# Layer 1's loop of a four-layer graph network: small results moved out of a shared PSUM bank, two sums moved to VectorE, and the steps of a turn put in another order

## The chip, the cores and the metric

The kernel is one program on one core of a Trainium2 chip. The core has five engines that run side by side, each through its own list of instructions in order: TensorE (PE, matmuls; its weight loads are listed as PEld), VectorE (DVE), ScalarE (ACT), GpSimd (POOL) and SyncE (SP, which here only starts DMA transfers). An engine waits on a semaphore until another has finished what it needs. Matmul results land in PSUM, everything else lives in SBUF. The metric is the device time of one execution in microseconds (us); before the change it was 1585.68 us, the median of three runs.

## The reference, cut to what matters

Eight batches of 2048 nodes with 64 features run through four graph layers, each closed by a residual sum and a layer norm. The change touches only layer 1:

```python
h = x @ W
# agg: for each of 64 hyperedges, a softmax-weighted sum of the h of its members
beta = sigmoid((h @ a_gn)[:, None, :] + (agg @ a_ge)[:, :, None])
all_he = elu(beta * h + (1 - beta) * agg)          # one row per (hyperedge, node) pair
industry = (adj / deg) @ (x @ W_ind)
coefs1 = softmax over a node's hyperedges of tanh(elu(agg) @ fcW + fcb) @ av
g = sum over hyperedges of coefs1 * all_he
pair = [industry, g]
coefs2 = softmax(tanh(pair @ fcW + fcb) @ av)       # two weights per node and batch
out = coefs2[0] * industry + coefs2[1] * g
x = layernorm(x + out)                               # over 64 features
```

A node belongs to few hyperedges. The kernel handles the first three memberships of each node as three "units", and further ones as a list of slots; unit 3 is such a slot, put back to its node by a matmul with a selection matrix `S`.

## The kernel before: the parts that the change touches

Layer 1's loop works on tiles of 128 nodes, 16 of them (`j` = 0 to 15); a tile is 128 partitions by 512 columns (8 batches of 64 features). Four generators describe the work on one tile: `units` (the gated hyperedge terms, result `g`), `industry` (the big product with the adjacency mask, 32 matmuls in 8 blocks of 4, each block one step `i`), and `mix_and_norm` (the two-way softmax and the layer norm). A string of steps says how one turn of the loop interleaves them; each engine then gets its instructions in exactly that order.

```python
bank = ps_s.tile([P, QW], F32, tag="bank", name="bank")        # ONE 128x512 PSUM tile for all small things
def units(j, dst):
    sm = bank[:, 208 * (j % 2):208 * (j % 2 + 1)]
    ...  # step sx: 3 small matmuls and a transpose of S[:, j] into sm
    nc.scalar.copy(ST, sm[:, 0:P])                             # step ST
    nc.scalar.copy(of_slot..., sm[:, P + 64:P + 80])
    ex = sm[:, P:P + 64]...                                    # step gates: 4 small VectorE ops read ex
    ...                                                        #   and write gate, coef (SBUF)
    tau = sm[:, 0:4 * B]...                                    # step tau: the gates' tanh goes BACK into the bank
    nc.scalar.activation(tau, gate, AF.Tanh, scale=0.5)
    for i in range(2):
        ...  # gp{i}: 4 matmuls into gp (2 banks, one buffer)
        # z{i}: three VectorE ops on 128x1024: d = h + 1 - gp ; d *= tau + 1 (reads the bank) ; d = d / 2 + gp
        # (for i = 1 the first two are on half, the other half comes from step t3: 8 ScalarE ops from dp)
        # exp{i}: ScalarE, gp <- exp(d - 1) ; e{i}: VectorE, ez <- max(min(gp, 1), d)
        # w{i}: GpSimd, ez *= coef (for i = 0 also g = ez[0] + ez[1])
    nc.gpsimd.tensor_tensor(g, g, w[1][:, 0], ALU.add)         # step g1
    nc.tensor.matmul(mv, ST, w[1][:, 1], ...)                  # step red
    nc.vector.tensor_tensor(g, g, mv, ALU.add)                 # step g
def mix_and_norm(j):
    nc.sync.dma_start(xr, kept[j])                             # step xg
    nc.gpsimd.tensor_tensor(r, g, xr, ALU.add)
    # for ind, then g: tr{i} 4 transposes, sT{i} ScalarE copy, fc{i} 2 matmuls (shown as 4), th{i} ScalarE tanh
    # sub: GpSimd, th[0] -= th[1]
    df, sw, s, rp = (bank[:, 416 + 48 * (j % 2) + k * B:][:, 0:B] for k in range(4))
    # df: 8 matmuls of one column into the bank ; sw: ScalarE tanh, bank to bank ; dlt: VectorE ind -= g
    # mix: VectorE: ind *= sw + 1 ; r += ind / 2 ; s = sum of r (into the bank) ; r -= s / 64 (reads the bank)
    # sq: ScalarE square ; var: VectorE sum ; rstd: GpSimd, 2 ops
    nc.scalar.copy(rp, rstd)                                   # step rp, into the bank
    nc.vector.tensor_tensor(x2[:, j, :], r, bcast(rp), ALU.mult)   # step x2
turns = (
    "u.gp0 u.z0 s.g1 s.red p.i o.df f.rstd m.xg s.g u.exp0 o.sw f.rp u.dp m.tr0 f.x2 "
    "u.e0 u.w0 o.dlt p.i u.gp1 u.t3 m.sT0 u.z1 p.i m.fc0 m.th0 u.exp1 o.mix v.sx v.ST "
    "o.sq m.tr1 m.sT1 p.i u.e1 u.w1 o.var v.gates v.tau p.i m.fc1 m.th1 m.sub p.i p.i p.i"
)
# in turn t:  p -> industry of t, u -> units of t+1, v -> units of t+2, s -> units of t,
#             m, o, f -> mix_and_norm of t-1, t-2, t-3
```

Of the kernel before, what the change touches and what calls it, by code (L numbers as in the profile page):

```python
# [18 lines left out]
P = 128  # L19
# [3 lines left out]
BC = B * C  # L23
# [26 lines left out]
def kernel(  # L50
# [53 lines left out]
    def b_view(t2):  # L104
        return t2.rearrange("p (b c) -> p b c", b=B)
# [299 lines left out]
    def layer1(  # L405
# [28 lines left out]
        with tc.tile_pool(name="fa", bufs=2) as fa, tc.tile_pool(  # L434
# [201 lines left out]
            for j in range(NT):  # L636
# [6 lines left out]
        fw = stack.enter_context(tc.tile_pool(name="fw", bufs=2))  # L643
        mjp = stack.enter_context(tc.tile_pool(name="mj1", bufs=2))
        turn = {}
        homes = {"g": (0, 1, 2, 3), "ind": (4, 5, 14), "sT": (6, 7), "r": (8, 9, 10),
                 "xr": (12,), "sq": (13,)}

        def row(tag, name):
            turn[tag] = turn.get(tag, -1) + 1  # L650
            home = homes[tag][turn[tag] % len(homes[tag])]
            return own.tile([P, BC], F32, tag=f"b1_{home}", name=name)

        def small(tag, name, shape=(P, B), bufs=2):
            return fw.tile(list(shape), F32, tag=tag, name=name, bufs=bufs)
# [4 lines left out]
        ps_g = stack.enter_context(tc.tile_pool(name="fg", bufs=1, space=PSUM))  # L660
        ps_m = stack.enter_context(tc.tile_pool(name="fm", bufs=2, space=PSUM))
        ps_s = stack.enter_context(tc.tile_pool(name="fs", bufs=1, space=PSUM))

        bank = ps_s.tile([P, QW], F32, tag="bank", name="bank")
        ps_acc = stack.enter_context(tc.tile_pool(name="fi", bufs=1, space=PSUM))
        ps_fc = stack.enter_context(tc.tile_pool(name="ff", bufs=1, space=PSUM))
        extv = ext.rearrange("p u k b -> p (u k b)")


        def units(j, dst):  # L670

            cols = slice(j * P, (j + 1) * P)
            sm = bank[:, 208 * (j % 2):208 * (j % 2 + 1)]

            for i in range(2):
                nc.tensor.matmul(
                    sm[:, P + 32 * i:P + 32 * i + 32], (oh01, oh23)[i][:, cols], extv,
                    start=True, stop=True,
                )
            nc.tensor.matmul(  # L680
                sm[:, P + 64:P + 80], S[:, j, :], hgr[:, j].rearrange("p k b -> p (k b)"),
                start=True, stop=True,
            )
            transpose(sm[:, 0:P], S[:, j, :])
            yield "sx"
            ST = small("ST", f"ST_{j}", (P, P), 3)
            nc.scalar.copy(ST, sm[:, 0:P])
            of_slot = small("of_slot", f"of_slot_{j}", (P, 2, B))
            nc.scalar.copy(of_slot.rearrange("p k b -> p (k b)"), sm[:, P + 64:P + 80])
            yield "ST"  # L690
            ex = sm[:, P:P + 64].rearrange("p (u k b) -> p u k b", u=4, k=2)
            gate = small("gate", f"gate_{j}", (P, 4, B))
            coef = small("coef", f"coef_{j}", (P, 4, B), 3)
            for t, k, op in ((gate, 0, ALU.add), (coef, 1, ALU.mult)):
                nc.vector.tensor_tensor(
                    t[:, 0:3, :], ex[:, 0:3, k, :],
                    hgr[:, j, k, :].unsqueeze(1).to_broadcast([P, 3, B]), op,
                )
                nc.vector.tensor_tensor(t[:, 3, :], ex[:, 3, k, :], of_slot[:, k, :], op)
            yield "gates"  # L700

            tau = sm[:, 0:4 * B].rearrange("p (u b) -> p u b", u=4)
            nc.scalar.activation(tau, gate, AF.Tanh, scale=0.5)
            tau3 = small("tau3", f"tau3_{j}")
            nc.scalar.activation(tau3, tau[:, 3, :], AF.Copy, bias=1.0)
            yield "tau"


            def per_b(t, u, n):
                return (  # L710
                    t[:, u:u + n, :].rearrange("p u b -> p (u b)").unsqueeze(2)
                    .to_broadcast([P, n * B, C])
                )

            def by_b(t):
                return t.rearrange("p u (b c) -> p (u b) c", b=B)

            w = []
            for i in range(2):
                gp = ps_g.tile([P, 2, BC], F32, tag="g", name=f"gp_{j}_{i}")  # L720
                for u in range(2):
                    rs = slice(u * 64, (u + 1) * 64)
                    for part in (agg_hi, agg_lo):
                        nc.tensor.matmul(  # L724
                            gp[:, u, :], r_((oh01, oh23)[i][rs, cols]), r_(part[rs]),
                            start=part is agg_hi, stop=part is agg_lo,
                        )
                yield f"gp{i}"
                d = small("d", f"d_{j}_{i}", (P, 2, BC))
                n = 2 - i  # L730
                if i == 1:
                    for b in range(B):
                        bc = slice(b * C, (b + 1) * C)
                        nc.scalar.activation(
                            d[:, 1, bc], dp[:, bc], AF.Copy, scale=tau3[:, b:b + 1]
                        )
                    yield "t3"
# [4 lines left out]
                nc.vector.scalar_tensor_tensor(  # L742
                    by_b(d[:, 0:n]), per_b(tau, 2 * i, n), 1.0, by_b(d[:, 0:n]),
                    op0=ALU.add, op1=ALU.mult,
                )
                nc.vector.scalar_tensor_tensor(d, d, 0.5, gp, op0=ALU.mult, op1=ALU.add)  # L746
                yield f"z{i}"
                nc.scalar.activation(gp, d, AF.Exp, bias=minus1)
                yield f"exp{i}"
                if i == 0:  # L750

                    dp = ps_m.tile([P, BC], F32, tag="m", name=f"dp_{j}")
                    nc.tensor.matmul(dp, S[:, j, :], h_sb[:, j, :], start=True, stop=False)  # L753
# [5 lines left out]
                    yield "dp"  # L759
                ez = small("ez", f"ez_{j}_{i}", (P, 2, BC))  # L760
# [30 lines left out]
        def mix_and_norm(j):  # L791
# [31 lines left out]
            df, sw, s, rp = (  # L823
                bank[:, 416 + 48 * (j % 2) + k * B:][:, 0:B] for k in range(4)
            )
            for b in range(B):
                nc.tensor.matmul(  # L827
                    df[:, b:b + 1], th[0][:, b % 2, (b // 2) * P:(b // 2 + 1) * P], av_sb,
                    start=True, stop=True,
                )  # L830
# [10 lines left out]
            nc.vector.scalar_tensor_tensor(  # L841
                b_view(r), bcast(s), -1.0 / C, b_view(r), op0=ALU.mult, op1=ALU.add
            )
# [25 lines left out]
        second = "gp0 z0 exp0 dp e0 w0 gp1 t3 z1 exp1 e1 w1"  # L869
# [826 lines left out]
```

## Time and profile before

| what | value |
|---|---|
| time, median of 3 runs | 1585.68 us (1582.55 to 1592.32) |
| span of the profiled execution | 1586.5 us |
| PE busy, share of the span | 1396.5 us, 88% |
| DVE busy | 897.3 us, 57% |
| ACT busy | 296.4 us, 19% |
| POOL busy | 347.6 us, 22% |
| granted TensorE clock, whole span | 0.905 |
| layer 1's loop, from the first block of the mask product to layer 2 | about 869 to 1280 us |

How to read it. Busy time is an average over stages that have different limits, so it says little about one stage. A busy PE is not a PE at full speed, as its clock is granted in two levels and the same matmul takes longer at the lower one. A group line names the kernel's line, the engine, the operation and the tiles (out<-in). "Idle before" is the time in which that engine stood still just before the instruction, and "<-" names whose end let it go on. A line of the stage table gives the stage, its length, the busy time of each engine in it (with the number of instructions in brackets), the granted clock, and the DMA's share and rate.

### The profile page before, as it was taken

Reading aid. Unit: us, or ns where it says so; the run is one execution under the profiler, and the core shown is the slowest. Engines: PE = TensorE matmul, PEld = TensorE weight load, DVE = VectorE, ACT = ScalarE, POOL = GpSimd, SP = SyncE. Lnnn points to the kernel's source line nnn. Section 1 sums busy time; section 2 is a strip of 40 time slices with the busy share of each in tenths; the row PEclk is TensorE's granted clock in tenths of the full one; section 3 lists DMA queues with packets and bytes.
Section 4 is the critical chain, followed back from the end, with each engine's and each line's share of the span. In section 5 each row is a group of like instructions: output and inputs, shape, how many; then the busy total and the mean of one; then the engine's idle time right before and its main releaser. Section 6 shows DMA issues by size and latency. Waiting matters only on the chain.

```text
span 1586.5 us, 19276 instructions
## 1 busy us (share of the span) xinstructions
PE 1396.5 (88%) x7552; PEld 1074.8 (68%) x7552; DVE 897.3 (57%) x1627; ACT 296.4 (19%) x700; POOL 347.6 (22%) x245
## 2 busy tenths in 40 slices
PE   6877959999999999994877988888888879999997
PEld 4666748888888888882654555555555568888886
DVE  6655405665665666575764555555555466565554
ACT  2100100001001000001331433333333322111111
POOL 3344411011000100000001535353545432000000
PEclk9989979999999999995995977788787889999999
DMA  7555191112212211002001212121212032343562
GB/s 266 225 212 212 53 207 55 48 55 74 60 52 64 74 48 33 22 8 51 1 7 54 67 33 67 34 67 33 67 34 67 7 80 81 109 130 107 173 185 95
DMA packets 166707, 131.51 MB, mean 83 GB/s; under 512 B 12208, under 2 KB 151888, under 8 KB 162256
## 3 DMA queue, kind: packets, MB, share of 16 engines
q1 hardware_dynamic: 146496, 100.68, 21.4%
q10 hardware_dynamic: 19872, 28.94, 5.3%
q8 instruction: 62, 1.02, 0.3%
q0 software_dynamic: 240, 0.56, 0.1%
q14 instruction: 37, 0.30, 0.1%
HBM read 104.99 MB, written 25.17 MB: 82 GB/s over the span
## 4 chain that ended last, share of the span: by engine, by line
PE 68%; DVE 11%; issue 3%; DMA 2%; ACT 2%; POOL 1%; ACTq 1%; SPq 0%; DVEq 0%; POOLq 0%
PE pp L175 20%; PE a L927 15%; PE ind L927 7%; PE y2p L927 7%; PE hp L556 2%; PE bank L827 2%; PE u L1031 2%; DVE d L742 2%; DVE d L738 2%; PE gp L724 2%; PE trm L149 1%; PE fc L815 1%; PE try L149 1%; DVE d L746 1%; PE dp L753 1%
## 5 line engine op out<-in xcount | busy, mean ns | idle before, releaser
L186 DVE SCALAR_TENSOR_TENSOR r<-pp,emb_sb,r 128x256 f32<-128x256 f32 x512 | 247.7, 484 | 107.9 <-PE pp L175 94.1
L175 PE MATMUL pp<-w_sb,xT 64*128 64x256 f32 x1024 | 157.6, 382 | 16.6 <-DMA xT<-in_xt 14.2
L175 PE MATMUL pp<-w_sb,y1T 64*128 64x256 f32 x1024 | 157.4, 381 | 0.0
L175 PE MATMUL pp<-w_sb,y2T 64*128 64x256 f32 x1024 | 155.7, 378 | 0.0
L927 PE MATMUL ind<-y_hi,mj_l 128*128 128x512 f32 x256 | 133.0, 520 | 0.0
L175 PEld LDWEIGHTS pp<-w_sb,xT 64*128 64x128 f32 x1024 | 100.0, 188 | 32.5 <-DMA xT<-in_xt 14.6
L351 PE MATMUL y1p<-x_hi,m 128*128 128x512 f32 x256 | 107.7, 421 | 10.9 <-DVE m L318 10.9
L927 PE MATMUL ind<-y_lo,mj_l 128*128 128x512 f32 x256 | 116.9, 457 | 0.0
L351 PE MATMUL y1p<-x_lo,m 128*128 128x512 f32 x256 | 107.0, 418 | 4.1 <-DVE x_lo L301 4.1
L175 PEld LDWEIGHTS pp<-w_sb,y2T 64*128 64x128 f32 x1024 | 101.7, 188 | 9.6
L175 PEld LDWEIGHTS pp<-w_sb,y1T 64*128 64x128 f32 x1024 | 100.5, 188 | 10.5 <-issue 0.5
L763 POOL TENSOR_TENSOR ez<-ez,coef 128x1024 f32<-128x1024 f32 x32 | 65.8, 2056 | 184.8 <-DVE ez L761 125.7
L738 DVE SCALAR_TENSOR_TENSOR d<-h,gp 128x1024 f32<-128x1024 f32 (+1 forms) x32 | 30.6, 955 | 132.5 <-PE gp L724 132.5
L927 PE MATMUL y2p<-y_hi,mj_y 128*128 128x512 f32 x256 | 103.4, 404 | 0.4 <-DMA mj_y<-mask 0.4
L927 PE MATMUL a<-y_lo,mj_l 128*128 128x512 f32 x256 | 103.5, 405 | 0.0
L927 PE MATMUL a<-y_hi,mj_l 128*128 128x512 f32 x256 | 102.8, 402 | 0.0
L927 PE MATMUL y2p<-y_lo,mj_y 128*128 128x512 f32 x256 | 102.5, 400 | 0.0
L341 POOL TENSOR_TENSOR ms<-m,sb 128x2048 f32<-128x2048 f32 x16 | 78.6, 4912 | 106.7 <-ACT sb L331 68.9
L927 PE MATMUL a<-v_hi,mj_l 128*128 128x512 f32 x256 | 99.9, 391 | 0.0
L927 PE MATMUL a<-v_lo,mj_l 128*128 128x512 f32 x256 | 99.7, 390 | 0.0
L927 PEld LDWEIGHTS ind<-y_hi,mj_l 128*128 128x128 f32 x256 | 59.6, 233 | 35.1 <-issue 23.9
L953 POOL TENSOR_TENSOR y<-y_hi,y_lo 128x512 f32<-128x512 f32 x16 | 20.5, 1284 | 265.2 <-PE try L149 265.0
(246 smaller groups left out, 2354.1 us busy)
## 6 DMA issues: line engine op xcount, KB each, us to landing
mj_l<-mask SPq DMA_DIRECT2D x192, 256.0 KB, 3.9
raw<-in_at SPq DMA_DIRECT2D x16, 1024.0 KB, 5.9
mask<-m ACTq DMA_DIRECT2D x16, 1024.0 KB, 5.9
mj_y<-mask SPq DMA_DIRECT2D x64, 256.0 KB, 3.9
xraw<-in_xn SPq DMA_DIRECT2D x4, 1024.0 KB, 6.3
xs<-in_xn SPq DMA_DIRECT2D x16, 256.0 KB, 2.9
xT<-in_xt ACTq DMA_DIRECT2D x16, 256.0 KB, 2.9
kept<-x SPq DMA_DIRECT2D x16, 256.0 KB, 2.0
```

The costliest lines, as they stand in the source:

```text
L149: nc.tensor.matmul(dst, src, ident, start=True, stop=True, is_transpose=True)
L175: nc.tensor.matmul(pp[:, h, pl, :], src[rs, 2 * bq + pl, ncols], w_sb[rs, k, dq * 4 * C:(dq + 1) * 4 * C], start=k == 0, stop=k == K - 1,)
L186: nc.vector.scalar_tensor_tensor(rb, ppv[:, :, dd, :], emb_sb[:, j, d:d + 1], rb, op0=ALU.mult, op1=ALU.add,)
L341: nc.gpsimd.tensor_tensor(ms, m, sb[:, qc].unsqueeze(1).to_broadcast([P, 4, QW]), ALU.mult)
L351: nc.tensor.matmul(accs[jj], r_(m[:, mm, jj * P:(jj + 1) * P]), r_(part[:, 4 * kk + mm, :]), start=i == 0 and mm == 0 and part is x_hi, st ...
L556: nc.tensor.matmul(mm[:, i, 0:2 * P + 4], xT[:, 2 * p2 + i, :], wb, start=True, stop=True)
L724: nc.tensor.matmul(gp[:, u, :], r_((oh01, oh23)[i][rs, cols]), r_(part[rs]), start=part is agg_hi, stop=part is agg_lo,)
L738: nc.vector.scalar_tensor_tensor(d[:, 0:n], h_sb[:, j, :].unsqueeze(1).to_broadcast([P, n, BC]), 1.0, gp[:, 0:n], op0=ALU.add, op1=ALU.sub ...
L742: nc.vector.scalar_tensor_tensor(by_b(d[:, 0:n]), per_b(tau, 2 * i, n), 1.0, by_b(d[:, 0:n]), op0=ALU.add, op1=ALU.mult,)
L763: nc.gpsimd.tensor_tensor(by_b(ez), by_b(ez), per_b(coef, 2 * i, 2), ALU.mult)
L827: nc.tensor.matmul(df[:, b:b + 1], th[0][:, b % 2, (b // 2) * P:(b // 2 + 1) * P], av_sb, start=True, stop=True,)
L927: nc.tensor.matmul(acc, r_(a[:, mt, :]), r_(part[:, mt, :]), start=mt == 0 and part is hi, stop=mt == NT - 1 and part is lo,)
```

## The change

It keeps the arithmetic's result and alters where small things lie, which engine does some of them, and the order of a turn:

- The shared bank is gone. The small matmuls of `sx` and of `df` each get a PSUM tile of their own time (one buffer for both in turn). ScalarE copies all 80 small columns to SBUF at once (`ex`); the gates, their tanh (`tau`, now in place over `gate`), `sw`, the norm's sum `s` and `rstd` stay in SBUF.
- Two GpSimd sums go to VectorE: the last sum of `g` and the residual's sum with `xr`.
- The last product of the norm (`x2`) goes from one VectorE op to eight ScalarE ops (one per batch, with `rstd` as the scale), and the copy `rp` goes.
- `t3` comes before `e0`, `mix` is cut into `mult`, `r` and `centre`, one block of the mask product stands between `fc0` and `sx`, and the row `xr` is loaded a turn earlier into one of two buffers.

```diff
-        homes = {"g": (0, 1, 2, 3), "ind": (4, 5, 14), "sT": (6, 7), "r": (8, 9, 10),
-                 "xr": (12,), "sq": (13,)}
+        homes = {"g": (0, 1, 2, 3), "ind": (5, 14), "sT": (7, 4), "r": (8, 9, 10),
+                 "xr": (6, 12), "sq": (13,)}
-        bank = ps_s.tile([P, QW], F32, tag="bank", name="bank")
-            sm = bank[:, 208 * (j % 2):208 * (j % 2 + 1)]
+            sm = ps_s.tile([P, QW], F32, tag="sm", name=f"sx_{j}")
-            of_slot = small("of_slot", f"of_slot_{j}", (P, 2, B))
-            nc.scalar.copy(of_slot.rearrange("p k b -> p (k b)"), sm[:, P + 64:P + 80])
+            ex = small("ex", f"ex_{j}", (P, 5, 2, B))
+            nc.scalar.copy(ex.rearrange("p u k b -> p (u k b)"), sm[:, P:P + 80])
-            ex = sm[:, P:P + 64].rearrange("p (u k b) -> p u k b", u=4, k=2)
-            tau = sm[:, 0:4 * B].rearrange("p (u b) -> p u b", u=4)
+            tau = gate
 ... (d2 for i = 1 is taken early, so that step t3 can run after dp and before e0)
-            nc.gpsimd.tensor_tensor(g, g, w[1][:, 0], ALU.add)
-            yield "g1"
-            nc.vector.tensor_tensor(g, g, mv, ALU.add)
+            nc.vector.tensor_tensor(w[1][:, 0], w[1][:, 0], mv, ALU.add)
+            nc.vector.tensor_tensor(g, g, w[1][:, 0], ALU.add)
-            r = row("r", f"r1_{j}")
-            nc.gpsimd.tensor_tensor(r, g, xr, ALU.add)
-            yield "xg"
+            yield "xr"
-            df, sw, s, rp = (
-                bank[:, 416 + 48 * (j % 2) + k * B:][:, 0:B] for k in range(4)
-            )
+            df = ps_s.tile([P, QW], F32, tag="sm", name=f"df_{j}")[:, 0:B]
+            sw = small("sw", f"sw_{j}")
-            nc.vector.scalar_tensor_tensor(r, ind, 0.5, r, op0=ALU.mult, op1=ALU.add)
+            yield "mult"
+            r = row("r", f"r1_{j}")
+            nc.vector.scalar_tensor_tensor(r, ind, 0.5, g, op0=ALU.mult, op1=ALU.add)
+            nc.vector.tensor_tensor(r, r, xr, ALU.add)
+            yield "r"
+            s = small("s", f"s_{j}")
-            yield "mix"
+            yield "centre"
-            nc.scalar.copy(rp, rstd)
-            yield "rp"
-            nc.vector.tensor_tensor(b_view(x2[:, j, :]), b_view(r), bcast(rp), ALU.mult)
+            for b in range(B):
+                bc = slice(b * C, (b + 1) * C)
+                nc.scalar.activation(x2[:, j, bc], r[:, bc], AF.Copy, scale=rstd[:, b:b + 1])
-            "u.gp0 u.z0 s.g1 s.red p.i o.df f.rstd m.xg s.g u.exp0 o.sw f.rp u.dp m.tr0 f.x2 "
-            "u.e0 u.w0 o.dlt p.i u.gp1 u.t3 m.sT0 u.z1 p.i m.fc0 m.th0 u.exp1 o.mix v.sx v.ST "
-            "o.sq m.tr1 m.sT1 p.i u.e1 u.w1 o.var v.gates v.tau p.i m.fc1 m.th1 m.sub "
-            "p.i p.i p.i"
+            "m.xr u.gp0 s.red u.z0 f.rstd s.g p.i u.exp0 o.df o.sw u.dp m.tr0 u.t3 m.sT0 p.i u.e0 "
+            "u.w0 o.dlt o.mult u.gp1 f.x2 u.z1 p.i m.fc0 m.th0 u.exp1 o.r p.i v.sx v.ST m.tr1 "
+            "m.sT1 u.e1 u.w1 o.centre o.sq v.gates v.tau p.i m.fc1 p.i m.th1 m.sub p.i o.var p.i"
```

More of the change, by code (lines that the diff above doesn't have):

```diff
@@ L698, in units @@
                 )
-                nc.vector.tensor_tensor(t[:, 3, :], ex[:, 3, k, :], of_slot[:, k, :], op)
+                nc.vector.tensor_tensor(t[:, 3, :], ex[:, 3, k, :], ex[:, 4, k, :], op)
             yield "gates"
-            tau = sm[:, 0:4 * B].rearrange("p (u b) -> p u b", u=4)
+            tau = gate
             nc.scalar.activation(tau, gate, AF.Tanh, scale=0.5)
@@ L728, in units @@
                 yield f"gp{i}"
-                d = small("d", f"d_{j}_{i}", (P, 2, BC))
+                if i == 0:
+                    d, d2 = (small("d", f"d_{j}_{k}", (P, 2, BC)) for k in range(2))
+                else:
+                    d = d2
                 n = 2 - i
[L731 to L735, printed above, removed]
-                        )
-                    yield "t3"
                 nc.vector.scalar_tensor_tensor(
@@ L759, in units @@
                     yield "dp"
+                    for b in range(B):
+                        bc = slice(b * C, (b + 1) * C)
+                        nc.scalar.activation(
+                            d2[:, 1, bc], dp[:, bc], AF.Copy, scale=tau3[:, b:b + 1]
+                        )
+                    yield "t3"
                 ez = small("ez", f"ez_{j}_{i}", (P, 2, BC))
@@ L822, in mix_and_norm @@
             yield "sub"
-            df, sw, s, rp = (
-                bank[:, 416 + 48 * (j % 2) + k * B:][:, 0:B] for k in range(4)
-            )
+            df = ps_s.tile([P, QW], F32, tag="sm", name=f"df_{j}")[:, 0:B]
             for b in range(B):
@@ L854, in mix_and_norm @@
             yield "rstd"
-            nc.scalar.copy(rp, rstd)
-            yield "rp"
-            nc.vector.tensor_tensor(b_view(x2[:, j, :]), b_view(r), bcast(rp), ALU.mult)
+            for b in range(B):
+                bc = slice(b * C, (b + 1) * C)
+                nc.scalar.activation(x2[:, j, bc], r[:, bc], AF.Copy, scale=rstd[:, b:b + 1])
             yield "x2"
@@ L868, in layer1 @@
         first = "sx ST gates tau"
-        second = "gp0 z0 exp0 dp e0 w0 gp1 t3 z1 exp1 e1 w1"
+        second = "gp0 z0 exp0 dp t3 e0 w0 gp1 z1 exp1 e1 w1"
         turns = (
-            "u.gp0 u.z0 s.g1 s.red p.i o.df f.rstd m.xg s.g u.exp0 o.sw f.rp u.dp m.tr0 f.x2 "
-            "u.e0 u.w0 o.dlt p.i u.gp1 u.t3 m.sT0 u.z1 p.i m.fc0 m.th0 u.exp1 o.mix v.sx v.ST "
-            "o.sq m.tr1 m.sT1 p.i u.e1 u.w1 o.var v.gates v.tau p.i m.fc1 m.th1 m.sub "
-            "p.i p.i p.i"
+            "m.xr u.gp0 s.red u.z0 f.rstd s.g p.i u.exp0 o.df o.sw u.dp m.tr0 u.t3 m.sT0 p.i u.e0 "
+            "u.w0 o.dlt o.mult u.gp1 f.x2 u.z1 p.i m.fc0 m.th0 u.exp1 o.r p.i v.sx v.ST m.tr1 "
+            "m.sT1 u.e1 u.w1 o.centre o.sq v.gates v.tau p.i m.fc1 p.i m.th1 m.sub p.i o.var p.i"
         )
```

## The prediction

> **What bounds the kernel now.** I read first the stages, with one turn of layer 1's loop per stage. A turn starts where the first block of `gp` matmuls starts. Each row gives the stage and its length, then PE, PEld, DVE, ACT and POOL busy, the granted clock and the DMA.
>
> ```profile
> 881.73:899.03 17.30, 15.89 (x70) 9.47 (x69) 9.64 (x13) 8.31 (x19) 9.50 (x7) 1.00 0.27 77
> ...
> 1059.76:1086.21 26.45, 22.46 (x87) 13.53 (x86) 14.11 (x20) 9.22 (x22) 12.28 (x9) 0.81 0.18 50
> 1086.21:1111.41 25.20, 20.98 (x87) 13.39 (x86) 14.11 (x20) 9.31 (x22) 12.22 (x9) 0.86 0.18 53
> ...
> 1216.33:1238.56 22.23, 19.98 (x80) 12.32 (x80) 13.69 (x16) 8.61 (x18) 12.12 (x9) 0.85 0.21 60
> ```
>
> No other engine is busy for more than 14.11 of some 26 us, so PE's list sets the turn. Turns 2 to 13 run from 899.03 to 1216.33: 317.3 us, 26.44 each. Turn 1 (first row), which has no `df` and nothing of the residual and norm yet, takes 17.30 us at full clock. What fills the other 9? I asked what PE waited for in those twelve turns (total, times, longest):
>
> ```profile
> PE bank L676 <- DVE r L841: 38.2, 12, 3.5
> PE bank L827 <- DVE d L742: 9.3, 12, 0.8
> ```
>
> The first line is `sx` (it writes `bank`) waiting for the norm's centring, a VectorE op that reads its own eight columns of the same bank. The second is `df` waiting for the second op of `z0`, which reads `tau` in the bank. Neither is a dependence of data. That is 38.2/12 = 3.18 and 9.3/12 = 0.78, together 3.96 us a turn. The rest shows in PE's instructions of turn 8 (start, length, engine, what; the wait in brackets):
>
> ```profile
> 1062.08 0.39 PE L927 MATMUL ind<-y_lo,mj_l 128*128 128x512 f32 x1
> 1063.27 1.92 PE L827 MATMUL bank<-av,th 128*128 128x1 f32 x16 [0.80 <-DVE d L742]
> 1065.05 1.69 PE L753 MATMUL dp<-h,S 128*128 128x512 f32 x2
> ...
> 1070.01 0.63 PE L927 MATMUL ind<-y_lo,mj_l 128*128 128x512 f32 x1
> ...
> 1072.54 0.40 PE L927 MATMUL ind<-y_hi,mj_l 128*128 128x512 f32 x1
> 1073.10 1.13 PE L815 MATMUL fc<-sT,fcw_sb 64*128 64x512 f32 x4
> 1077.42 0.63 PE L676 MATMUL bank<-ext,oh 128*128 128x32 f32 x4 [3.19 <-DVE r L841]
> ...
> 1080.91 0.63 PE L927 MATMUL ind<-y_hi,mj_l 128*128 128x512 f32 x1
> 1081.33 0.63 PE L927 MATMUL ind<-y_lo,mj_l 128*128 128x512 f32 x1
> ```
>
> After each wait the same 128x512 matmul goes from 0.40 to 0.63 us (starts 0.43 apart, not 0.23). So a wait is paid twice: as idle time and as a slow clock after it.
>
> **What the Trainium skill says.** "PSUM — Partial Sum Buffer", section "PSUM bank collisions raise a hardware error": accesses of different engines have to be kept apart by bank, not by address. The trace agrees: `sx` at columns 0 to 415 waits 3.2 us for an op on columns above 416. "TensorE: Matmul & The Clock Gate", Part 1: the clock falls to half after a window of about 3.4 us without enough activity and rises after one busy window. The trace agrees: slow stretches follow the 3.2 us wait and the stretch of `df` with its wait, spacing 0.43 against 0.23. "ScalarE: Activation LUTs", section "What ACT_TABLE_LOAD costs": 186 ns, plus 93 for a pointer operand, plus 0.833 per element, less 93 of overlap back to back; for 64 columns I estimate 239 ns an op from it. The trace's eight alike ops (`d<-dp`) take 1.74 us, 218 each; I use that. "GPSIMD Engine Reference", section 3.1: a two-input elementwise op is about twice as slow there as on VectorE. Here 1278 ns against 681 for 128x512.
>
> **The change, part by part.**
>
> *The floor of a PE turn.* Turn 1 holds two waits, 1.04 us (`g`) and 0.37 (`e0`): 17.30 - 1.41 = 15.9. Add `df`: without a wait, in turn 15, it runs from 1240.53 to 1242.23, so 1.7. The block moved between `fc0` and `sx` makes one more change between the two kinds of matmul, each about 0.35 us of PEld "issue". Floor: 15.9 + 1.7 + 0.35 = 18.0 us. So the old average of 26.44 is 17.6 + 3.96 of waits + 0.2 more in `df` + some 4.7 of slow clock.
>
> *Removed.* With `tau`, `s`, `sw` and `rstd` in SBUF and `ex` copied by ScalarE, the tile of `sx` and `df` has readers on ScalarE alone: `sw` (done some 7 us before `sx`) and the two copies. Both waits go, 3.96 us a turn.
>
> *Moved between engines.* VectorE gains two sums of 0.69 and loses `x2` (0.69): 14.1 to 14.8 us. GpSimd loses 1.28 + 1.27: 12.2 to 9.7. ScalarE loses `rp` (0.17) and gains eight ops (1.74): 9.3 to 10.9. None reaches 18, so what counts is whether a chain through them is late.
>
> *The chains, laid out by hand at 18 us, from the start of `gp0`.* VectorE: `z0` 0.8 to 4.6 (three of 1.22, as now), the two sums of `g` to 5.9, under ScalarE's `exp0` (4.7 to 5.8), `e0` to 7.2. PE reaches `gp1` at about 7.5, so this just fits. ScalarE: `t3` from 6.1 to 7.9, `sT0` to 8.5 (`fc0` comes at 9.3), `x2` to 10.3, `th0` 10.5 to 11.6, `exp1` to 12.7 (`z1` ends at 11.35), the copies of `sx` and `sT1` to 13.75, `fc1` at 13.85: tight. VectorE: `r` to 12.75, `e1` 12.8 to 14.0, `centre` to 15.4, `gates` to 15.9. ScalarE: `sq`, `tau` to 16.4, `th1` to 17.55. GpSimd: `sub` (2.4) to 20.0; the next turn's `df` comes at 18.0 + 2.55 = 20.5. Nothing stands in PE's way for long, though four places have under 0.6 us to spare. I allow 0.4 us a turn.
>
> *Clock.* The slow stretch after `sx` has lost its cause. That after `df` may stay, as 16 one-column matmuls do little. In turn 14, with the wait, it came; in turn 15, where `df` followed without a wait, the matmuls after it still took 0.39. I expect it in about a third of the turns, 2.7 us each: 0.9.
>
> *Sum.* 18.0 + 0.4 + 0.9 = 19.3 us a turn, 7.1 less, over 12 turns 85 us. Turn 14 loses a wait of 0.78 and part of a slow stretch: -2. Turns 0 and 1 gain a change of matmul kind: +0.7. At the end of the loop layer 2's first copy on VectorE no longer stands behind the wait for the last `rstd` (2.09 us), but one VectorE sum was added: -1. Together -87: 1585.7 - 87 = 1499; I say 1500.
>
> **The rivals.**
>
> 1. *The slow clock stays.* If `df` alone sets it off in each turn, 2.7 us instead of 0.9: 18.0 + 0.4 + 2.7 = 21.1, 64 us saved, about 1520. For it: turn 14 had no wait at `sx`, and yet a clock of 0.85. Against: turn 15.
> 2. *A wait takes the place of the old one.* `gp1` on `e0`, `fc1` on `sT1` or `df` on `sub` could each be late by 0.5 to 1 us, most likely `fc1`: in turn 14 it waited 1.47 us for `sT1`. There `sq` stood ahead of `sT1`; in the new order it stands behind. If two are late by a microsecond, with half the slow stretches left: 18.0 + 2 + 1.5 = 21.5, 1525.
> 3. *The mask's load becomes late.* The load of `xr` stands ahead of the next mask in SyncE's list. Its buffer is free after `r` (12.75) only, where the mask's four loads now start at a turn's begin. Started at 13 and landing 3.9 us later, the first quarter is there at 17.5 to 18; it is needed at 19.2. So hidden, but with less to spare; if not, a wait of 1 to 2 us, 1525.
> 4. *VectorE becomes the bound.* At 14.8 of 18 us it is not, unless chains line up badly; that is rival 2.
>
> **Range and chances.** With no slow clock and no leftover wait the turn is 18.0: 12 x 8.4 + 2 = 103 saved, 1483. With rivals 1 and 2 together (22 us a turn) it is 1532. So 1482 to 1532. Staying within 2% (above 1554) needs a turn of over 23.8, which would keep two thirds of the loss: unlikely. Slower needs a new stall of over 10 us a turn, and nothing points at one. Faster by over 2%: 0.95; within: 0.04; slower: 0.01.
>
> **What the profile after will show.** Right: no PE wait for the centring or for `z0` at `sx` and `df`; turns 2 to 13 of 18 to 21 us; a clock of the loop above 0.90; VectorE near 14.8 us a turn; unchanged stages before 869 us. Wrong: turns above 22 us, PE waiting for `sT`, `sub` or the mask's load, or a clock still at 0.81 although the waits are gone.

## The result and the profile after

After the change the kernel takes **1522.08 us** (median of 4, 1519.46 to 1524.41); the kernel before took 1586.11 us in the same series (median of 4). The ratio is **0.9592**, 95% interval 0.9557 to 0.9627: 4.1% faster, some 64 us. The profiled execution spans 1522.7 us at a clock of 0.925 (before: 1586.5 us at 0.905).

The stages of the kernel after, one turn each, in the columns used before (stage and length, then PE, PEld, DVE, ACT and POOL busy, clock, DMA):

```profile
946.49:966.68 20.19, 17.96 (x86) 11.06 (x86) 18.85 (x22) 10.80 (x30) 11.05 (x6) 1.00 0.24 66
966.68:986.99 20.31, 18.07 (x87) 11.08 (x86) 19.07 (x22) 11.02 (x31) 11.05 (x6) 1.00 0.22 66
1007.27:1029.12 21.85, 21.18 (x86) 12.88 (x86) 18.95 (x22) 10.90 (x31) 11.04 (x6) 0.84 0.21 61
...
1049.31:1069.62 20.31, 19.62 (x87) 12.13 (x86) 19.08 (x22) 11.02 (x31) 11.05 (x6) 0.92 0.23 66
```

Turns 2 to 13 run from 905.63 to 1151.52: 245.9 us, 20.49 each, where they were 26.44. Compare the second row with the last: at a clock of 1.00 PE is busy for 18.07 us, at 0.92 for 19.62, and both turns take 20.31. PE has slack in the first and so no longer sets the turn. VectorE is busy for 19.1 us in both, not 14.8, though it does only what it was meant to do: 252 instructions in the twelve turns, 21 in each, where it was 20 (one that straddles the end of a turn is counted in both rows). Its own waits from 905 to 1130 us, eleven turns, (total, times, longest) leave it idle for some 1.5 us a turn:

```profile
DVE d L730 <- PE gp L720: 12.5, 13, 4.2
DVE var L848 <- ACT sq L845: 3.6, 10, 0.4
```

So **VectorE's list now bounds most turns**, though not by itself: the chain of the turn at 966.68 runs through VectorE's ops from 967.46 to 980.94, then through `exp1` and `sT1` on ScalarE to `fc1` (982.93) and 3 us of mask product on PE, back to the next `gp0`. PE's waits, from 840 to 1230 us, show both old bank waits gone and two for late results in their place:

```profile
PE df L820 <- POOL th L816: 10.6, 14, 1.7
PE fc L810 <- ACT sT L805: 9.9, 8, 1.9
```

Why does VectorE take longer? Here are lines from the turn at 966.68 of the kernel after (start, length, engine, what). Each VectorE op shown stands beside a GpSimd op:

```profile
967.79 2.38 POOL L816 TENSOR_TENSOR th<-th,th 128x1024 f32<-128x1024 f32 x1 [2.65 <-ACT th L813]
968.79 2.46 DVE L734 SCALAR_TENSOR_TENSOR d<-gate,d 128x1024 f32<-128x1024 f32 x1
970.12 1.22 POOL L850 TENSOR_SCALAR var<-var 128x8 f32<-128x8 f32 x1
970.22 1.95 PE L820 MATMUL df<-av,th 128*128 128x1 f32 x16 [0.68 <-POOL th L816]
975.05 2.28 POOL L761 TENSOR_TENSOR ez<-ez,coef 128x1024 f32<-128x1024 f32 x1 [1.96 <-DVE ez L759]
975.67 2.21 DVE L830 SCALAR_TENSOR_TENSOR ind<-sw,ind 128x512 f32<-128x512 f32 x1
982.93 1.13 PE L810 MATMUL fc<-sT,fcw_sb 64*128 64x512 f32 x4 [1.57 <-ACT sT L805]
983.53 1.90 POOL L761 TENSOR_TENSOR ez<-ez,coef 128x1024 f32<-128x1024 f32 x1 [4.48 <-DVE ez L759]
984.02 1.97 DVE L840 SCALAR_TENSOR_TENSOR r<-s,r 128x512 f32<-128x512 f32 x1
986.02 0.63 ACT L845 ACTIVATE sq<-r 128x512 f32<-128x512 f32 x1 [3.14 <-DVE r L840]
```

In the kernel before, the same four ops (`mult`, the centring and the second ops of `z0` and `z1`) took this long in turns 2 to 13 (count, then busy us, mean ns):

```profile
L742 DVE SCALAR_TENSOR_TENSOR d<-bank,d 128x1024 f32<-128x1024 f32 x12 | 14.7, 1225 | 1.2
L742 DVE SCALAR_TENSOR_TENSOR d<-bank,d 128x512 f32<-128x512 f32 x12 | 8.3, 691 | 0.5
L841 DVE SCALAR_TENSOR_TENSOR r<-bank,r 128x512 f32<-128x512 f32 x12 | 8.3, 691 | 0.4
L836 DVE SCALAR_TENSOR_TENSOR ind<-bank,ind 128x512 f32<-128x512 f32 x12 | 8.2, 685 | 0.0
```

The second op of `z0` (L734) starts at 968.79, inside GpSimd's `sub` (967.79 to 970.17), and ends at 971.25: 1.1 us after `sub`, as if it had begun only then. It took 1.22 before. The `mult` (L830) ends 0.55 us after `w0` and takes 2.21 instead of 0.69. The centring (L840) ends 0.56 us after `w1` and takes 1.97 instead of 0.69. With 1.01 instead of 0.69 for the half op of `z1` (mean of its group) that is 1.24 + 1.52 + 1.28 + 0.32 = **4.4 us in such a turn** (4.1 in the mean of the twelve, as `z0` is not always hit in full), which the profile counts as busy time. It goes the other way too: GpSimd's small addition to `var` (L850), issued while L734 runs, takes 1.22 us; alone it takes 0.24.

These four ops have one thing in common: their small operand (`tau`, `sw`, `s`) lay in PSUM before and lies in SBUF now. The Trainium skill, "SBUF — State Buffer", section "Who interferes with whom", says what that may do: a VectorE instruction with two inputs in SBUF contends with a GpSimd instruction that reads SBUF, not with one that only writes there, and whichever was issued first holds the shared port until it is done. One more hint is L836 (`r` + `xr`), which also reads two tiles in SBUF: at 981.57 GpSimd is idle, and it takes 0.69.

From there to PE's waits the way is short. A late centring makes `sq`, `th1` and `sub` late, so `sub` meets `z0` and `df` waits 0.68. A late `mult` pushes `z1` back, then `exp1` (ScalarE, 980.96), then `sT1` behind it, and `fc1` waits 1.57.

**Theory "ports".** The separation of banks took the old waits away; putting `tau`, `sw` and `s` into SBUF, of all places outside the bank, made VectorE share its way to SBUF with GpSimd, which stretches the chain through its list to 20.3 us, 2.3 above PE's floor. **Rivals:** the two sums that VectorE took over make its list too long; or the new order puts `sT1` and `sub` too late by itself; or `df` keeps the clock slow whatever is done.

### The profile page after: what moved, and what is told of

It is laid out like the page before. It is cut to its first block, busy times and chain, and to the rows that moved or that the text cites. A ratio compares the mean times of both kernels' runs of the same rounds, so it can differ in the third digit from the quotient of the medians.

```text
span 1522.7 us, 19336 instructions
## 1 busy us (share of the span) xinstructions
PE 1364.3 (90%) x7552; PEld 1051.2 (69%) x7552; DVE 965.9 (63%) x1643; ACT 323.3 (21%) x812; POOL 325.3 (21%) x213
## 4 chain that ended last, share of the span: by engine, by line
PE 63%; DVE 11%; ACT 4%; issue 3%; DMA 2%; POOL 2%; ACTq 1%; SPq 0%; DVEq 0%; POOLq 0%
PE pp L175 21%; PE a L925 15%; PE y2p L925 7%; PE ind L925 4%; PE hp L556 2%; PE u L1029 2%; DVE d L734 2%; PE fc L810 1%; PE try L149 1%; PE df L820 1%; POOL th L816 1%; DVE ind L830 1%; DVE d L738 1%; DVE d L730 1%; PE yp L1055 1%
## 5 line engine op out<-in xcount | busy, mean ns | idle before, releaser
L175 PE MATMUL pp<-w_sb,xT 64*128 64x256 f32 x1024 | 158.3, 383 | 18.5 <-DMA xT<-in_xt 16.1
L925 PE MATMUL ind<-y_hi,mj_l 128*128 128x512 f32 x256 | 118.5, 463 | 0.7 <-ACT ind L783 0.7
L351 PE MATMUL y1p<-x_hi,m 128*128 128x512 f32 x256 | 107.5, 420 | 10.7 <-DVE m L318 10.7
L925 PE MATMUL ind<-y_lo,mj_l 128*128 128x512 f32 x256 | 106.7, 417 | 0.0
L925 PEld LDWEIGHTS ind<-y_hi,mj_l 128*128 128x128 f32 x256 | 52.0, 203 | 48.0 <-issue 30.9
L956 ACT COPY y1T<-try 128x512 f32<-128x512 f32 x16 | 9.4, 587 | 332.2 <-PE try L149 298.4
```

What stands on the lines that cost most here:

```text
L175: nc.tensor.matmul(pp[:, h, pl, :], src[rs, 2 * bq + pl, ncols], w_sb[rs, k, dq * 4 * C:(dq + 1) * 4 * C], start=k == 0, stop=k == K - 1,)
L351: nc.tensor.matmul(accs[jj], r_(m[:, mm, jj * P:(jj + 1) * P]), r_(part[:, 4 * kk + mm, :]), start=i == 0 and mm == 0 and part is x_hi, st ...
L925: nc.tensor.matmul(acc, r_(a[:, mt, :]), r_(part[:, mt, :]), start=mt == 0 and part is hi, stop=mt == NT - 1 and part is lo,)
```

## The experiments

Each ratio is to the kernel before, run on the same chip in the same series, with its 95% interval. Experiments are called by the numbers of their headings, 1 to 8; e1 to e10 are the single kernels.

### 1. The homes alone: e1_homes_only

The kernel before with the small things moved to SBUF and `sx` and `df` in a tile of their own; the old order, `x2` on VectorE and the sums on GpSimd stay.

```diff
-            sm = bank[:, 208 * (j % 2):208 * (j % 2 + 1)]
+            sm = ps_s.tile([P, QW], F32, tag="sm", name=f"sx_{j}")
-            tau = sm[:, 0:4 * B]...
+            tau = gate
+            df = ps_s.tile([P, QW], F32, tag="sm", name=f"df_{j}")[:, 0:B]
+            sw, s, rp = (small(k, f"{k}_{j}") for k in ("sw", "s", "rp"))
... (the old bank goes, and ScalarE copies `ex`, as in the change)
```

> The kernel before, with only the homes of the small results changed: sx and df in tiles of their own time, ex, tau, sw, s and the copied rstd in SBUF. Old order, sums on GpSimd, x2 on VectorE. Theory 'bank' (the waits at the shared bank were the whole loss): PE's waits for the centring and z0 go, 1520 to 1535 us. Theory 'ports' (a VectorE op with both tensors in SBUF stands still while GpSimd works, and the homes in PSUM avoided that): the waits go, but z0's second op, mult, the centring and x2 take up to 2 us longer each, and the old order puts them against GpSimd's work: 1535 to 1560. Theory 'order' (the new order of steps brings most): above 1560.

Measured: 1540.68 us, ratio 0.970 (0.9671 to 0.9729). No wait for the bank is left; PE waits for late results instead (900 to 1130 us):

```profile
PE fc L812 <- ACT sT L807: 21.1, 10, 2.3
PE gp L721 <- DVE ez L758: 6.1, 5, 1.4
```

The homes alone bring three quarters of the gain of the whole change (48 of 64 us). In the old order the centring and the `mult` still take 0.69, but the second op of `z0` takes 1.74 and the half op of `z1` 1.46 us, and one more is hit: the first op of `gates`, which reads `ex` and a second tile in SBUF, takes 1.58 instead of 0.17. So the stretching comes with the homes, and the order decides which ops it hits.

### 2. The bank shared again in the new order: e2_shared_bank

```diff
+        bank = ps_s.tile([P, QW], F32, tag="bank", name="bank")
-            sm = ps_s.tile([P, QW], F32, tag="sm", name=f"sx_{j}")
+            sm = bank[:, 208 * (j % 2):208 * (j % 2 + 1)]
-            tau = gate
+            tau = sm[:, 0:4 * B]...
+            df, sw, s = (bank[:, 416 + 48 * (j % 2) + k * B:][:, 0:B] for k in range(3))
... (their tiles in SBUF and the tile of `df` go)
```

> The kernel after, with tau, sw and s back in one PSUM bank shared with sx and df, as before; order, sums and x2 stay as after. Theory 'bank': PE waits at sx and df for VectorE again, above 1550 us. Theory 'ports' together with 'order': in the new order sx stands ahead of the centring, so only df's wait for z0 (0.8 us a turn) comes back; z0's second op goes from 2.46 to 1.22 us, mult from 2.21 to 0.69, the centring from 1.97 to 0.69, and the time is 1500 to 1515, below the kernel after.

Measured: 1519.23 us, 0.9558 (0.9535 to 0.9581): the same as the change, and 4 us above what was expected. VectorE's ops are back at 1.22, 0.69 and 0.69 us. The wait of `sx` does not come back, because the new order puts `sx` ahead of the centring. That of `df` does (`z0` still reads `tau` in the bank), and the slow clock comes with it (PE's wait from 900 to 1130 us, then three turns):

```profile
PE bank L823 <- DVE d L735: 8.5, 11, 0.8
904.35:922.86 18.51, 17.74 (x86) 11.14 (x86) 15.41 (x21) 9.01 (x21) 6.19 (x4) 1.00 0.26 72
922.86:944.44 21.58, 20.78 (x86) 12.89 (x86) 15.41 (x21) 10.93 (x30) 9.76 (x6) 0.84 0.20 61
944.44:966.09 21.65, 20.89 (x86) 12.83 (x85) 15.40 (x21) 11.00 (x30) 9.76 (x6) 0.84 0.22 62
```

So two different losses of equal size hide behind one time: a bank wait of 0.8 us with its slow clock here, stretched ops in the kernel after.

### 3. A bank that PE never writes: e3_own_bank

`tau`, `sw` and `s` in a PSUM bank without matmuls; `sx` and `df` go into the tile of `fc`, so as to free that bank.

```diff
+        bank = ps_s.tile([P, QW], F32, tag="bank", name="bank")
-            sm = ps_s.tile([P, QW], F32, tag="sm", name=f"sx_{j}")
+            sm = ps_fc.tile([P, 2, BC], F32, tag="fc", name=f"sx_{j}")[:, 0]
-            df = ps_s.tile([P, QW], F32, tag="sm", name=f"df_{j}")[:, 0:B]
+            df = ps_fc.tile([P, 2, BC], F32, tag="fc", name=f"df_{j}")[:, 0, 0:B]
-            tau = gate
+            tau = bank[:, 32 * (j % 2):32 * (j % 2) + 32]...
-            sw = small("sw", f"sw_{j}")
+            sw = bank[:, 64 + B * (j % 2):64 + B * (j % 2) + B]
-            s = small("s", f"s_{j}")
+            s = bank[:, 96 + B * (j % 2):96 + B * (j % 2) + B]
```

> The kernel after, with tau, sw and s in a PSUM bank that TensorE never writes; sx and df use fc's banks instead. No wait for the old bank can come back, and no op of VectorE reads these small tensors from SBUF. Theory 'ports': z0's second op 1.22 us, mult and centring 0.69, VectorE busy 15 us a turn in place of 19, turns of 18.3 to 19.3 us, 1490 to 1510 us. Theory 'bank' alone (nothing lost to ports): as the kernel after, 1522.

Measured: **1493.40 us, 0.9385** (0.9346 to 0.9424), 33 us less than the change by the two ratios. Two of its turns, then the groups of VectorE's ops from 905 to 1120 us (count, then busy us, mean ns):

```profile
904.63:922.56 17.93, 17.78 (x86) 11.15 (x85) 15.32 (x21) 9.22 (x21) 6.56 (x5) 1.00 0.25 74
1015.51:1034.99 19.48, 19.32 (x87) 11.96 (x86) 15.40 (x21) 11.11 (x29) 9.77 (x7) 0.91 0.23 68
```

```profile
L735 DVE SCALAR_TENSOR_TENSOR d<-bank,d 128x1024 f32<-128x1024 f32 x12 | 14.7, 1225 | 1.2
L831 DVE SCALAR_TENSOR_TENSOR ind<-bank,ind 128x512 f32<-128x512 f32 x12 | 8.3, 692 | 1.3
L841 DVE SCALAR_TENSOR_TENSOR r<-bank,r 128x512 f32<-128x512 f32 x11 | 7.6, 691 | 0.4
```

The same ops on the same amount of data, with only the small operand elsewhere. One small op is still held here: the first of `gates`, with both inputs in SBUF, takes 0.84 us instead of 0.17. Nine of twelve turns take 17.92 to 18.00 us: the floor of 18.0 that the prediction worked out. The other three have a slow stretch and take 19.5.

### 4. The two sums back on GpSimd: e4_pool_sums

```diff
-            nc.vector.tensor_tensor(w[1][:, 0], w[1][:, 0], mv, ALU.add)
-            nc.vector.tensor_tensor(g, g, w[1][:, 0], ALU.add)
+            nc.gpsimd.tensor_tensor(g, g, w[1][:, 0], ALU.add)   # ahead of red
+            nc.vector.tensor_tensor(g, g, mv, ALU.add)
-            nc.vector.tensor_tensor(r, r, xr, ALU.add)
+            nc.gpsimd.tensor_tensor(r, g, xr, ALU.add)           # step xg
```

> The kernel after, with the two sums back on GpSimd (g plus w, and r as g plus xr). If VectorE's work as such limits the turn, 1.4 us less of it there makes it faster: 1508 to 1515. Theory 'ports': GpSimd is busy 2.55 us longer a turn, so VectorE's ops with two SBUF tensors meet it more often, and rstd, w0 start later: 1525 to 1545.

Measured: 1530.12 us, 0.9634 (0.9611 to 0.9657). VectorE has two ops fewer and the kernel is not faster. The stretching stays (`z0` 2.34, `mult` 2.21, centring 1.97 us), one more op is hit (`dlt`, 1.14 instead of 0.68), and where the sums stood VectorE now waits for ScalarE's `exp` (900 to 1130 us):

```profile
DVE ez L759 <- ACT gp L740: 16.0, 22, 1.4
```

The sums had filled a gap. A turn at full clock still takes 19.96 us. As GpSimd also reads SBUF for longer here, this run alone does not settle what the sums cost; experiment 8, where the four ops are not stretched, does, and there that rival falls.

### 5. GpSimd made short, or made to write only: e5_pool_short and e5_pool_memset

Both keep the change's homes in SBUF. The first cuts `sub` and the products of `w0` and `w1` to 8 columns; the second puts two fills of the tile in place of each. Both leave the work of these three steps out, so their times are no times of a whole kernel.

```diff
-  nc.gpsimd.tensor_tensor(by_b(ez), by_b(ez), per_b(coef, 2 * i, 2), ALU.mult)
+  nc.gpsimd.tensor_tensor(ez[:, 0, 0:B], ez[:, 0, 0:B], coef[:, 2 * i, :], ALU.mult)   # e5_pool_short
+  for _ in range(2): nc.gpsimd.memset(ez, 0.25 * (i + 1))                             # e5_pool_memset
```

> The kernel after with all homes as they are (tau, sw, s in SBUF), but GpSimd's three large ops of a turn (the two products of ez with coef, and th minus th) done on 8 columns only; the rest of those products and of the difference is left out, so the time is not that of the whole computation. Theory 'ports' (GpSimd's work is what stops VectorE): z0's second op 1.22 us, mult 0.69, centring 0.69. If instead reading the broadcast small tensor from SBUF is slow in itself: 2.2, 2.2 and 2.0 us as in the kernel after.

> As the last, but each of those three large GpSimd ops is replaced by two fills of the same tile with a constant: GpSimd writes SBUF for as long or nearly, and reads none; the products and the difference are left out. If only GpSimd's reads stop VectorE's second SBUF operand: z0's second op near 1.22, mult and centring near 0.69 us even where they lie beside a fill. If writes stop it too: over 1.5 us where they meet.

Measured, one run each: 1474.44 and 1472.11 us. With short GpSimd ops, `z0`, `mult` and centring take 1.23, 0.69 and 0.69 us, though their operands lie in SBUF. The half op of `z1` still takes 1.03: in ten of twelve turns it begins inside GpSimd's first sum of `g`, which was left whole. That alone leaves two readings open: the port, or the earlier end of GpSimd's work. The fills tell them apart, as they keep GpSimd busy beside the same VectorE ops:

```profile
1000.22 1.97 POOL L762 MEMSET ez<- 128x1024 f32 x2 [3.09 <-DVE ez L759]
1000.73 0.69 DVE L842 SCALAR_TENSOR_TENSOR r<-s,r 128x512 f32<-128x512 f32 x1
1010.93 1.96 POOL L762 MEMSET ez<- 128x1024 f32 x2 [4.87 <-DVE ez L759]
1011.57 0.69 DVE L832 SCALAR_TENSOR_TENSOR ind<-sw,ind 128x512 f32<-128x512 f32 x1
```

Centring and `mult` run wholly inside a pair of fills of nearly 2 us and take 0.69. So a busy GpSimd does no harm here; a GpSimd that reads SBUF does. That is what the skill's section says.

### 6. Which operand matters: e6_tau_psum and e7_sw_s_psum

As number 3, but with only `tau` in the bank without matmuls (e6), or only `sw` and `s` (e7).

```diff
# e6_tau_psum
-            tau = gate
+            tau = bank[:, 32 * (j % 2):32 * (j % 2) + 32]...
# e7_sw_s_psum
-            sw = small("sw", f"sw_{j}")
+            sw = bank[:, 64 + B * (j % 2):64 + B * (j % 2) + B]
-            s = small("s", f"s_{j}")
+            s = bank[:, 96 + B * (j % 2):96 + B * (j % 2) + B]
```

> The kernel with the bank of its own, but only tau in it; sw and s in SBUF. Both ops that read tau go back to 1.22 and 0.69 us, mult (2.2) and centring (2.0) stay long. The centring delays sq, th1 and sub, so df still waits for sub or fc for sT in part: turns near 19 us, 1503 to 1513. If tau's op was the whole matter: 1493.

> The complement: sw and s in the bank of its own, tau in SBUF. Mult and centring are 0.69 us; the centring is no longer late, so sub ends about 1.3 us earlier and may not even meet z0's second op in full: turns near 18.5 us, 1495 to 1508. If tau's ops are what holds the turn: 1515 to 1522.

Measured: e6 1520.30 us, 0.9588 (0.9547 to 0.963), no gain over the change; e7 1489.00 us, 0.9387 (0.9338 to 0.9435), all of the gain. Both missed what was expected. In e7 `tau` lies in SBUF and the second op of `z0` still takes 1225 ns: with `mult` and centring on time, `sub` is early and that op starts just behind its end at 977.97:

```profile
975.59 2.38 POOL L817 TENSOR_TENSOR th<-th,th 128x1024 f32<-128x1024 f32 x1 [1.70 <-ACT th L814]
978.02 1.23 DVE L735 SCALAR_TENSOR_TENSOR d<-gate,d 128x1024 f32<-128x1024 f32 x1
```

Its next neighbour on GpSimd, `rstd`, waits for it instead (2.52 us, 1.67 in the kernel before), and nothing waits for `rstd`. In e6 the late centring still makes `sub` late, `df` waits 0.2 to 0.7 us, and the clock spoils what the freed `z0` saved:

```profile
924.72:946.83 22.11, 21.23 (x86) 12.47 (x86) 18.00 (x22) 11.47 (x30) 10.08 (x6) 0.85 0.20 59
946.83:965.49 18.66, 18.17 (x87) 11.07 (x86) 17.04 (x21) 10.31 (x30) 10.07 (x6) 1.00 0.26 71
```

The turn at full clock is 1.6 us shorter than in the kernel after, and those with a slow stretch, 20.0 to 22.1, make up for it. So the operands of `mult` and centring decide, because what follows them leads to `sub` and `df`.

### 7. The old order with its banks set apart: e8_old_order_own_bank and e10_old_order_two_steps

The kernel before, its order and its sums, with `tau`, `sw`, `s` and `rp` in a bank without matmuls, `sx` and `df` in the tile of `fc`, and the gates' inputs copied by ScalarE. The second takes over two steps of the new order:

```diff
-  "... u.exp1 o.mix v.sx v.ST o.sq m.tr1 m.sT1 p.i u.e1 ..."
+  "... u.exp1 o.mix p.i v.sx v.ST m.tr1 m.sT1 o.sq u.e1 ..."     # e10_old_order_two_steps
```

> The kernel before with nothing but its banks set apart: tau, sw, s and rp in a PSUM bank that PE never writes, sx and df in fc's banks, the inputs of the gates copied out by ScalarE; the old order of steps, the sums still on GpSimd. It tells the worth of the separation from that of the order. If the order has a worth of its own, fc1 still waits for sT by some 2 us and gp1 for e0 by about 1 in each turn, as with the homes moved alone: turns of 20 to 21.5 us and 1515 to 1535 us in all. If the order mattered only because VectorE's slowed ops were late in the old one, these waits shrink under 0.5 us and the time is 1490 to 1505 us.

> The kernel before with its banks set apart, as in the run before of this kind (turns of 19.65 us, of which 1.24 is a wait of sx for th0, made by the tile that sx now shares with fc), and of the new order only two steps: one block of the mask stands ahead of sx, and the copy sT1 ahead of sq. If the new order is worth no more than these two steps once VectorE does not stand still: turns of 17.9 to 18.3 us at full clock and 1488 to 1500 us. If more of the order is needed, fc1, gp1 or df wait by some 1 us a turn and it is 1503 to 1518 us.

Measured: e8 1518.40 us, 0.9566 (0.9546 to 0.9587). Separating the banks, with the four ops unstretched and in the old order, is thus worth as much as the whole change. The time lies between the two ranges expected. The waits for `sT` and `ez` of experiment 1 have all but gone (1.8 us in 3 waits are left), so they came at least in part from stretched ops. Another wait is the experiment's own, of `sx` for the tile that it now shares with `fc`: 14.7 us in 12 waits; it also gives the other engines more time ahead of `fc1`. e10 takes that wait away and gains less than the 1.3 us a turn: 1510.42 us, 0.9501 (0.9476 to 0.9526). Its turns:

```profile
963.41:982.33 18.92, 18.15 (x86) 11.09 (x86) 15.43 (x20) 9.32 (x23) 12.23 (x8) 1.00 0.24 71
982.33:1003.90 21.57, 21.09 (x86) 12.51 (x85) 15.43 (x20) 9.37 (x23) 12.19 (x8) 0.84 0.21 61
```

At full clock it is within a microsecond of the floor, but `df` waits 0.2 to 0.45 us for `sub` in nearly every turn, and every second turn or so runs partly at the slow clock. Neither run is free of the port trouble, though. `ex` lies in SBUF in both, and the first op of `gates` meets the product `w1` on GpSimd (in e10 from 905 to 1120 us; then ScalarE's wait for it, ahead of `th1` and so of `sub`):

```profile
L693 DVE TENSOR_TENSOR gate<-ex,hgr 128x24 f32<-128x24 f32 x10 | 15.6, 1560 | 0.0
ACT bank L701 <- DVE gate L697: 26.1, 10, 2.7
```

It took 0.17 us in the kernel before. These 1.4 us are more than `df` waits, so whether the rest of the new order is needed, or only this op stands in the way, was not separated.

### 8. The sums on GpSimd without the port trouble: e9_own_bank_pool_sums

As number 3 with the edit of number 4.

> The new order with tau, sw and s in a bank that PE never writes, and the two sums back on GpSimd. It tells what the move of the two sums is worth where VectorE's ops do not stand still. If it is worth little by itself (GpSimd has room in a turn of 18 us: some 12 us of work), 1493 to 1505 us. If GpSimd's later results hold up the chain to fc1 or to the centring, waits of about 1 us a turn come back and the time is 1507 to 1525 us. The half op of z1 should take 0.88 us or less either way.

Measured: 1489.66 us, **0.9384** (0.9362 to 0.9406), against 0.9385 with the sums on VectorE. Moving the two sums is worth nothing here; GpSimd has room for them (12.3 us of a turn of 18). The time is 3 us below the range expected.

## Why the prediction was right, and where it was not

The prediction said 1500 us, in a range of 1482 to 1532; 1522 lies in the range, and the direction and the first half of the mechanism hold: the bank waits went. Of the expected 86 us, 22 are missing, for a cause that the prediction did not have. That the time still fell inside the range is in part luck, as the range allowed for late results and a slow clock and not for stretched ops; and that it is almost the 1520 of rival 1 is chance. One sign that it named for being right, VectorE near 14.8 us, failed, and one that it named for being wrong came: PE waits for `sT` and `sub`. Its steps one by one:

- **What bounds the kernel, and the waits removed (3.96 us a turn): right.** PE's list sets the turn and no bank wait is left. Experiment 2 adds that the wait of `sx` would have gone by the new order alone; only that of `df` needed the new home of `tau`.
- **The floor (18.0 us): right.** 17.91 to 18.00 us in the undisturbed turns of experiments 3 (e3) and 8 (e9).
- **The clock (0.9 us a turn): right in kind, too small.** The twelve turns have eight slow stretches, two of 6.8 and six of 3.4 us. At half clock they cost PE half their length, 17 us or 1.4 a turn. But only the two turns at 0.84 (21.8 and 21.9 us) are long for it; at 0.92 most take the same 20.2 to 20.3 us as at 1.00, since VectorE takes longer anyway. Where PE bounds again (experiment 3), slow stretches make the turn 0.4 us longer in the mean.
- **VectorE at 14.8 us, with 0.4 us for leftover waits: the step that failed.** The prediction priced each moved op by its length in the kernel before, as if the home of an operand had no part in it. VectorE took 18.8 us a turn in the mean and 19.1 in most; the 4.0 to 4.3 more are the four ops that stood still (4.1 in the mean by their groups, 4.4 where all are hit), and the sums themselves cost what was said. So most turns are 20.3 us where the sum had 18.0 + 0.4, at a clock of 1.00 and of 0.92: 20.49 in the mean instead of 19.3. Hand-laid chains with 0.6 us to spare cannot bear ops that are 1.2 to 1.5 us longer.
- **ScalarE at 10.9 and GpSimd at 9.7 us:** ScalarE takes 10.7 in the mean of the twelve turns, nearly as said; GpSimd 10.7, a microsecond more, since its own ops are held by VectorE's (the addition to `var` takes 1.13 us in the mean instead of 0.25, the first sum of `g` 1.64 instead of 1.30).
- **The rivals.** Rival 2 (a wait takes the place of the old one, most likely at `fc1`, or `df` on `sub`) came at just these two places. The prediction's reason was `sq` ahead of `sT1`; the reason found is the stretched ops. Rival 1 (the slow clock stays in each turn) came in part: in the kernel after the clock falls at or after `df` in seven of twelve turns, mostly where PE has time to spare. In experiment 2, where `df` waits 0.8 us and PE bounds, it does cost time (21.6 us a turn against 18.5). Rival 3 fell: the mask's loads still start at the turn's begin, and PE never waits for them. Rival 4 (VectorE becomes the bound), put aside because of 14.8 of 18 us, is what the stage rows show, and rival 2's waits at PE are its other face.
- **Turn 14 (-2): right** (22.23 to 19.90 us). **Turns 0 and 1 (+0.7): too small**, 0.8 each, 1.6 together (turn 1 from 17.30 to 18.10).
- **The end of the loop (-1): half right.** From the end of the last `df` to layer 2's first matmul it is 1.5 us shorter (9.8 to 8.3), since `dlt` and `x2` no longer stand ahead of `mult` on VectorE. The first copy for layer 2 waits 2.09 us for the last `rstd` as before, though. And the stretch from the end of turn 14 to the end of that `df` is 3.7 us longer (the `df` of turn 15 waits 0.67 us, then runs for 2.79 us at the slow clock), which the prediction did not lay out: +2.2 in all.

In the profiled executions the missing part adds up so: the loop's twelve turns saved 71.4 instead of 85 (13.6), its end 3.2, turns 0, 1 and 14 together 0.6, layer 2 some 1, and the loop began 5 us later. The last does not look like an effect of the change: in the profiled executions of the two kernels and the eleven experimental kernels the loop's first `gp` starts anywhere from 849.2 to 858.2 us. The kernel before (851.6) stands near the low end, beside experiment 4 (852.3), which has the new homes and the new order; the kernel after starts at 856.6.

So the whole splits like this: banks set apart in the old order, 0.9566 (0.9501 with two steps of the new one); with the whole new order, 0.9384; sums on VectorE, no change (0.9385); `tau`, `sw` and `s` in SBUF, back up to 0.9592. Only the last two steps stand without a rival: one moves the sums alone, and the other, besides the three small tensors, only where `sx` and `df` lie, which e6 shows to bring nothing. In the step to 0.9384, more than the order changes: it also moves `x2` to ScalarE, takes away the wait for the shared tile that e8 brought, and shortens the held op of `gates`; how much of it is the order is not shown. The best versions, experiments 3 (e3), 6 (e7) and 8 (e9), beat both kernels.

## What to carry to other kernels

Set small results apart from PSUM banks that TensorE writes, but before sending them to SBUF look at which VectorE ops read them beside a second SBUF tile and what GpSimd reads at that moment; a PSUM bank without matmuls kept the bank waits and nearly all of the port trouble away here. When a group's mean time grows with the same shape and count, look for another engine's op that covers its start: a stall inside an op is booked as busy, and no list of waits shows it. When a chain is laid out by hand, ask of each moved operand which port it comes through, and of each small wait on PE what it does to the clock.

## What the hardware did that was not expected

- VectorE ops of 0.69 us took 1.97 to 2.21 us, and one of 1.22 us took 2.46, when they began while GpSimd read SBUF; they ended 0.55 to 1.1 us after GpSimd did, a little under their own undisturbed length. GpSimd is held in the same way: an addition on 128x8 took 1.22 us instead of 0.24, `rstd` 2.52 instead of 1.67. GpSimd's fills held nothing.
- A VectorE op on only 24 columns is held as well: the first op of `gates` took 1.56 to 1.58 us instead of 0.17 where it met `w1` (experiments 1 and 7).
- The clock changes on a grid. Here are slow stretches of the kernel after, cut where its clock record changes, and one of experiment 3 (the last row):

```profile
930.10:936.92 6.82, 6.82 (x17) 3.33 (x17) 5.66 (x6) 4.81 (x18) 4.80 (x3) 0.50 0.01 3
1012.02:1018.84 6.82, 6.82 (x19) 4.05 (x18) 6.31 (x6) 3.57 (x13) 4.79 (x3) 0.50 0.11 29
1035.91:1039.32 3.41, 3.41 (x11) 2.33 (x12) 3.31 (x4) 3.24 (x15) 1.93 (x1) 0.50 0.02 5
1076.87:1080.28 3.41, 3.41 (x12) 2.06 (x10) 3.31 (x3) 3.41 (x15) 2.28 (x1) 0.50 0.00 0
946.67:950.08 3.41, 3.41 (x12) 2.14 (x11) 2.23 (x3) 3.41 (x15) 2.31 (x2) 0.50 0.01 2
```

  Each lasts 3.41 us or twice that, and in the kernel after they start 0, 24, 31 and 43 times 3.413 us after 930.10; in the kernel before and in e1, e2, e3, e6, e9 and e10 the changes of the clock keep to the same step. The Trainium skill, "TensorE: Matmul & The Clock Gate", Part 1, has the activity counted in windows of about 3.4 us that run on by themselves; the trace agrees. So where in a window `df` falls matters, and not only the wait ahead of it. In the kernel after, `df` waits 0.67 to 0.69 us in each of nine turns in a row. Where it starts 1.2 or 1.9 us before a point of the grid, the clock falls at that point (two turns). Where it starts 0.5 to 1.0 us before one, so that wait and `df` are split over two windows, the clock does not fall (four turns). Where it starts within 0.3 us of one, the clock falls at the next point (three turns). In experiment 3 it falls in a quarter of the turns without any wait at `df`. How little PE must do in a window for the clock to fall was not measured.
